# A two-layer graph network in one launch: order of first loads, place of the third dense product, chunks begun in hop 1, last chunks of hop 2 by halves

## The chip, the core and the metric

The kernel runs on one core of a Trainium2 chip. A core has five engines, each with an instruction queue of its own: TensorE (PE; its weight loads are listed as PEld), VectorE (DVE), ScalarE (ACT), GpSimd (POOL) and SyncE (SP), which here only issues DMAs. Sixteen DMA engines move data between HBM and the core's memories; SP, ACT and POOL issue to them. The metric is the device time of one launch in microseconds (us). The kernel before took 850.22 us, the median of three runs (850.05 to 854.02).

## The reference

x is [8, 2048, 128], adj is a 2048 x 2048 matrix R with about 0.4% of its entries nonzero (random pairs in both directions and the diagonal), all in fp32. Layer 0 computes, cut to what matters:

```
res = si[:, :, None] + sj[:, None, :] + R[None] * w_r + g_b     # si = x @ w_i, sj = x @ w_j
x   = layernorm(x + einsum('bij,bjd->bid', res, x) @ weight + bias)
```

Layer 1 is a Chebyshev step with the same matrix given twice:

```
x1 = einsum('bnf,nw->bwf', x, R);  x2 = 2 * einsum('bnf,nw->bwf', x1, R) - x      # for A1 and for A2, both R
x  = layernorm(x + relu(concat([x, x1, x2, x1, x2]) @ Theta1 + bias))
```

## The kernel before

**Tiling.** The 2048 nodes are 16 chunks of 128, numbered 0 to 15. A chunk of x or of a result is a tile of 128 nodes by 8 x 128 columns (batches by features), 512 KB; a product into it takes two PSUM banks of 512 columns, a half of the batches each. Of the eight PSUM banks, 0 to 3 hold two pairs of sums that are taken in turn (`acc_pair`, line 321), 4 and 5 serve the third dense product (`acc2`) and other things, 6 and 7 take transposes in turn.

**Dense and listed rows.** Layer 0 is computed as R times Y, Y = x @ weight, plus terms of rank nine (`rank9`). For chunks 0 to 3 this product is dense: `full_rows` (lines 311 to 318) multiplies the transposed block rows of R, kept in `at4`, with Y, two matmuls of 512 columns per block, in the order `LAST` (line 308: 0 to 3, 8 to 15, 4 to 7). For the other twelve chunks R is sparse enough to work with lists: DVE finds for each chunk which groups of columns hold a nonzero, ranks them, and writes indices `idx`. A chunk then needs its own diagonal block ("own"), four gathers by rows of 32 ("T") and three of 64 and 128 ("H"). A gather is an indirect DMA that POOL issues, of 128 rows of 4 KB of Y (or later u, y), and the rows of R that belong to it are gathered too, from `rr_d`, into a staging buffer `st` of four slots (`get_job`, line 543); DVE masks them and copies them to `rct` and `rc` (`keep_job`, line 554). `next_job` (line 662) is a keep followed by a get, so a POOL gather into a slot waits for DVE to have kept what was there.

**First stage (lines 327 to 345).** R is read in 16 block rows of 1 MB through a ring of three slots in the order `R_ORDER`. For each, DVE reduces it to a mask (`mask_rows`), PE transposes its 16 blocks in groups of four, and ACT copies each group out of PSUM, scaled by w_r (`wr`). With every second block row a chunk of x is transposed (`x_t`), multiplied with weight and the two columns of g_w, all in the tile `wx` (`y_of`), and the dense products of chunks 0 and 1 advance by one block. The loads are issued by SP, in the order of the list `todo` (lines 196 to 202), by `pump` (line 216) as far as their slots are free. ACT issues the small constants at the top (`load_constants`, lines 115 to 124): ten DMAs for `wx` (two), `wr`, the scalar `gb`, the bias row `b0row` (four times), `b1bc`, and `th` with the five blocks of Theta1.

**Lists (lines 686 to 701 and 776 to 822).** The remaining eight chunks of x go through the same steps, with the list work between them; then the ranking of the second set of lists runs on DVE in eight rounds (`rounds2`), while PE does column sums and the rank-nine terms. `lists_end(1)` (line 796) turns the second lists into indices with small transposes on PE. After it DVE adds residuals to the sums of chunks 0 and 1 (`z_add`) and normalises them; the third dense product, in three pieces of 5, 6 and 5 blocks, follows; between the pieces DVE and POOL do `next_job`s, and `make_u` (line 647) transposes a normalised chunk and multiplies it with the combined Theta block for the inner hop, storing it to `u_d` by a DMA of ACT's. The fourth dense product follows in the same way, and hop 0 (lines 839 to 862), the listed rows of layer 0, chunk by chunk.

**The buffers of gathered rows.** After layer 0's dense products Y is no longer needed, and twelve of its chunks, `Y[:, LAST[:12]]` (line 709), become the slots of gathered rows, taken in turn. The first T gathers of hop 0 overwrite Y of chunks 0 to 3, so they wait until the fourth dense product has read those.

**Hops of layer 1 (lines 865 to 940).** With the two equal matrices, the two hops are y = x Th1 + R^T u (hop 1, from `u_d`, results stored to `y_d`) and out = layernorm(x + relu(x Th2 + R^T y + bias)) (hop 2). For a chunk, `begin` does the products with Theta (eight matmuls), the own block and the T rows; `listed(.., "H")` the H rows; `end` copies the sums out (hop 1), or, in hop 2, adds the transposed x, applies the relu and the layer norm on DVE and ACT, and stores by a DMA of ACT's, 512 KB. POOL issues gathers in the order: T of two chunks, then per chunk the H rows of this one and the T rows of the next. In hop 1 the H rows of the first chunk need all of u, with the last chunk's `make_u` (`between`).

**Order of the instructions.** Every instruction goes through a wrapper, `Tied` (line 72), that keeps the program's order on each engine, so all of them carry line 72 in the profile and are told apart by their tiles.

**Semaphores of the DMAs.** In the built program the DMAs that SP and ACT issue take eight completion semaphores in turn, and those that POOL issues take eight others. A DMA waits, on the queue that issues it, until the one eight before it has completed.

Of the kernel before, what the change touches and what calls it, by code (L numbers as in the profile page):

```python
# [18 lines left out]
def kernel(  # L19
# [22 lines left out]
    P = 128  # L42
# [71 lines left out]

    def load_constants():
        with nc.allow_non_contiguous_dma(reason="two columns of 128 numbers"):
            act.dma_start(out=wx[:, D:D + 2], in_=g_w[0:2 * D].rearrange("(t p) -> p t", p=P))
        act.dma_start(out=wx[:, 0:D], in_=weight)
        act.dma_start(out=wr, in_=g_w[2 * D:2 * D + 1][None, :].to_broadcast([P, 1]))
        act.dma_start(out=gb, in_=g_b[None, :].to_broadcast([P, 1]))  # L120
        for i in range(4):
            act.dma_start(out=b0row[:, i, :], in_=bias0[None, :])
        act.dma_start(out=b1bc[:, 0, :], in_=bias1[None, :].to_broadcast([P, D]))
        act.dma_start(out=th, in_=theta.rearrange("(m p) f -> p m f", p=P))

    ctx.enter_context(nc.allow_non_contiguous_dma(reason="512-byte rows of a block of 128 columns"))
    load_constants()
    epst = const.tile([P, 1], F32)
# [68 lines left out]
    for k in range(NC):  # L197
        todo.append(("a", k))
        if x_at(k) is not None:
            todo.append(("x", x_at(k)))  # L200
    todo += [("x", 8), ("s", 12), ("x", 9), ("s", 13), ("x", 10), ("x", 11), ("s", 14), ("x", 12)]
    todo += [("s", 15), ("x", 13), ("x", 14), ("x", 15)] + [("c", c) for c in T_ORDER]
# [13 lines left out]
    def pump():  # L216
        while todo:
            what, n = todo[0]
            if what == "a" and n < done["a"] + 3:
                sp.dma_start(out=am[n % 3], in_=adj[R_ORDER[n] * P:(R_ORDER[n] + 1) * P, :])  # L220
            elif what == "x" and n < done["x"] + 6:
                c = X_ORDER[n]
                xin[c] = load_x(c, ring[:, X_SLOT[n % 6]])
                if c < ND:
                    zs[c] = xin[c]
            elif what == "s" and done["a"] == NC:
                store_rt(n)
            elif what == "c" and done["a"] == NC:
                copies([n])
            else:  # L230
                return
            todo.pop(0)
# [92 lines left out]

    acc0, acc1 = acc_pair(), acc_pair()
    pump()
    for k, n in enumerate(R_ORDER):
        m = x_at(k)
# [464 lines left out]
    next_job()  # L794
    rounds2([7])
    lists_end(1)
    z_add(acc0, zs[0])
# [3 lines left out]

    acc2 = bank[4:6]
    full_rows(2, acc2, LAST[:5])
    next_job()
    next_job()
    make_u(0, zs[0], x1t[0], u_of[0], 0)
    layernorm(zs[1], "0_1")
    full_rows(2, acc2, LAST[5:11])
    next_job()
    make_u(1, zs[1], x1t[1], u_of[1], 0)  # L810
    next_job()
    full_rows(2, acc2, LAST[11:])
    si_t(2)
    rank9(2, acc2)
    z_add(acc2, zs[2])
    overflow()
    next_job()
    layernorm(zs[2], "0_2")
# [46 lines left out]
    def hop(i, src, order, there, between):  # L865
        def theta_rows(c):
            accs = acc_pair()
            for h in range(2):
# [7 lines left out]
        def end(c, accs):  # L876
# [13 lines left out]
            else:  # L890
# [3 lines left out]
                )  # L894

        def fetch(k):
            if k < NC:
                load_own(i, src, order[k], homes[order[k]], order[k] in there)

        def begin(k):  # L900
            accs.append(theta_rows(order[k]))
            own_rows(i, order[k], accs[k], False)
            listed(i, order[k], accs[k], "T")
# [9 lines left out]
        rows(1, "T")  # L913
        begin(0)
        between()
        begin(1)
        for k, c in enumerate(order):
            rows(k, "H")
            if k > 1:
                begin(k)  # L920
            fetch(k + 2)
            if k > 0:
                rows(k + 1, "T")
# [111 lines left out]
```

## Time and profile before

| what | value |
|---|---|
| timed runs, median (three) | 850.22 us (850.05 to 854.02) |
| the profiled execution's own time | 818.08 us |
| its span (first to last instruction) | 816.3 us |
| mean granted TensorE clock | 0.971 |
| busy: PE, PEld, DVE, ACT, POOL | 90%, 45%, 48%, 24%, 55% of the span |
| DMA: bytes, mean rate | 253.90 MB, 311 GB/s |

How to read it: times are microseconds from the start of the span, means of one instruction are nanoseconds. The profile shows one execution, and the timed runs are other executions, 32 us longer in the median. "Busy" is the share of the span in which an engine executed something; issuing a DMA doesn't count. The chain of work that ended last is followed back from the last instruction, at each step to what released it. In a group or a line of the timeline, the bracket holds the idle time before it and what ended that. A timeline line gives start, length, engine, operation, output and inputs. A DMA's share is a mean over the sixteen engines.

The stages of this execution, from the timeline:

| stage | from | to |
|---|---|---|
| first loads; PE waits for the first x | 0 | 16.48 |
| R in 16 block rows, 12.41 us for two of them with one x | 16.48 | 109.5 |
| last x chunks, lists | 109.5 | 206 |
| third dense product ends | | 232.7 |
| fourth dense product ends | | 262 |
| hop 0 | 275 | 425 |
| hop 1 | 425 | 614 |
| hop 2, with the last store landed at 814.25 | 614 | 816.3 |

### The profile page before, as it was taken

Reading aid. Unit: us, or ns where it says so; the run is one execution under the profiler, and the core shown is the slowest. Engines: PE = TensorE matmul, PEld = TensorE weight load, DVE = VectorE, ACT = ScalarE, POOL = GpSimd, SP = SyncE. Lnnn points to the kernel's source line nnn. Section 1 sums busy time; section 2 is a strip of 40 time slices with the busy share of each in tenths; the row PEclk is TensorE's granted clock in tenths of the full one; section 3 lists DMA queues with packets and bytes.
Section 4 is the critical chain, followed back from the end, with each engine's and each line's share of the span. In section 5 each row is a group of like instructions: output and inputs, shape, how many; then the busy total and the mean of one; then the engine's idle time right before and its main releaser. Section 6 shows DMA issues by size and latency. Waiting matters only on the chain.

```text
span 816.3 us, 10067 instructions
## 1 busy us (share of the span) xinstructions
PE 732.8 (90%) x3554; PEld 364.9 (45%) x3554; DVE 394.7 (48%) x591; ACT 192.7 (24%) x439; POOL 445.2 (55%) x432
## 2 busy tenths in 40 slices
PE   4999999997999998988798888898899999999992
PEld 4666566642644343434345243333344454444441
DVE  4664876578341655555533000000100377777775
ACT  3757554321200332313222000000000011111101
POOL 1000000477747876776344677776774777776740
PEclk9999999997999999999899899999999999999997
DMA  8999999999326799999969799899999799999982
GB/s 264 296 314 316 352 292 295 314 398 347 119 89 223 244 346 368 341 344 367 356 224 344 246 364 360 314 365 346 339 372 357 252 343 357 370 385 389 363 299 68
DMA packets 165299, 253.90 MB, mean 311 GB/s; under 512 B 17255, under 2 KB 118020, under 8 KB 163192
## 3 DMA queue, kind: packets, MB, share of 16 engines
q0 software_dynamic: 49280, 146.52, 49.7%
q1 hardware_dynamic: 93200, 81.01, 31.1%
q10 hardware_dynamic: 22760, 25.63, 8.9%
q8 instruction: 30, 0.49, 0.2%
q14 instruction: 29, 0.24, 0.1%
HBM read 234.82 MB, written 58.72 MB: 360 GB/s over the span
## 4 chain that ended last, share of the span: by engine, by line
PE 52%; DMA 29%; issue 6%; ACT 6%; DVE 3%; POOL 2%; ACTq 0%; POOLq 0%; SPq 0%; DVEq 0%
PE bank L72 52%; DMA Y<-u_d,idx 12%; DMA Y<-y_d,idx 8%; DMA st<-rr_d,idx 2%; DMA rd<-rr_d 2%; ACT Y L72 2%; DMA ring<-in_x_dram 2%; POOL Y L72 1%; ACT rct L72 1%; ACT trp L72 1%; DMA trp<-in_adj_dram,idr 1%; DVE s L72 1%; DVE ring L72 1%; ACT at L72 1%; DVE st L72 1%
## 5 line engine op out<-in xcount | busy, mean ns | idle before, releaser
L72 POOL DMA_INDIRECT Y<-y_d,idx x196 | 212.0, 1081 | 93.2 <-PE bank L72 38.0
L72 PE MATMUL bank<-Y,rc 128*32 128x512 f32 (+2 forms) x896 | 219.7, 618 | 21.3 <-DMA Y<-u_d,idx 19.1
L72 POOL DMA_INDIRECT st<-rr_d,idx x84 | 90.3, 1075 | 183.5 <-DVE rown L72 148.3
L72 POOL DMA_INDIRECT Y<-u_d,idx x112 | 111.8, 999 | 53.9 <-issue 29.9
L72 PEld LDWEIGHTS bank<-Y,rc 128*32 128x32 f32 (+2 forms) x896 | 58.6, 130 | 179.3 <-issue 99.5
L72 PE MATMUL bank<-Y,at 128*128 128x512 f32 x256 | 115.2, 601 | 0.0
L72 PE MATMUL bank<-Y,rct 128*32 128x512 f32 (+2 forms) x336 | 77.3, 625 | 8.5 <-DMA Y<-y_d,idx 8.5
L72 DVE TENSOR_REDUCE s<-sq 128x4 f32<-128x512 f32 x64 | 43.9, 686 | 58.0 <-ACT sq L72 58.0
L72 PEld LDWEIGHTS bank<-Y,at 128*128 128x128 f32 x256 | 47.8, 193 | 53.6 <-issue 53.4
L72 DVE COPY ring<-bank 128x512 f32<-128x512 f32 x10 | 6.9, 692 | 110.1 <-PE bank L72 110.1
L72 ACT ACTIVATE sq<-ring 128x512 f32<-128x512 f32 x44 | 27.7, 630 | 129.5 <-DVE ring L72 109.7
L72 PE MATMUL bank<-ring,rd 128*128 128x512 f32 x108 | 51.5, 599 | 5.7 <-DMA rd<-rr_d 4.1
L72 PE MATMUL bank<-ident,rc 128*128 128x128 f32 (+2 forms) x302 | 45.0, 297 | 12.6 <-DMA rc<-in_adj_dram 6.6
L72 PE MATMUL bank<-th,at 128*128 128x128 f32 x384 | 49.2, 283 | 1.9 <-ACT at L72 1.9
L72 PEld LDWEIGHTS bank<-th,at 128*128 128x128 f32 x384 | 46.8, 197 | 6.7 <-ACT at L72 3.8
L72 DVE TENSOR_TENSOR ring<-bank,ring 128x512 f32<-128x512 f32 x26 | 17.3, 688 | 66.0 <-PE bank L72 60.8
L72 DVE TENSOR_REDUCE st<-rc 128x64 f32<-128x2048 f32 x16 | 36.5, 2283 | 25.7 <-DMA rc<-in_adj_dram 25.7
L72 ACT COPY ring<-bank 128x512 f32<-128x512 f32 x34 | 19.9, 586 | 122.5 <-PE bank L72 112.9
L72 PEld LDWEIGHTS bank<-Y,rct 128*32 128x32 f32 (+2 forms) x336 | 20.8, 130 | 57.3 <-issue 32.4
L72 PEld LDWEIGHTS bank<-ident,rc 128*128 128x128 f32 (+2 forms) x302 | 33.8, 150 | 25.5 <-issue 9.1
L72 PE MATMUL bank<-wx,trp 128*128 128x130 f32 x256 | 36.9, 288 | 4.3 <-ACT trp L72 2.2
L72 PE MATMUL bank<-ident,ring 128*128 128x128 f32 x232 | 32.5, 282 | 6.4 <-DMA ring<-in_x_dram 2.8
(142 smaller groups left out, 789.1 us busy)
## 6 DMA issues: line engine op xcount, KB each, us to landing
rc<-in_adj_dram SPq DMA_DIRECT2D x16, 1024.0 KB, 10.9
ring<-in_x_dram SPq DMA_DIRECT2D x25, 512.0 KB, 8.5
rr_d<-in_adj_dram SPq DMA_DIRECT2D x12, 1024.0 KB, 10.8
rr_d<-Y SPq DMA_DIRECT2D x8, 1024.0 KB, 9.0
y_d<-Y SPq DMA_DIRECT2D x16, 512.0 KB, 10.6
u_d<-ring ACTq DMA_DIRECT2D x12, 512.0 KB, 7.0
ring<-y_d SPq DMA_DIRECT2D x11, 512.0 KB, 23.2
ring<-u_d SPq DMA_DIRECT2D x10, 512.0 KB, 3.9
```

The source lines that it names most:

```text
L72: return lambda *a, **k: tc.keep_in_program_order(f(*a, **k))
```

## The change

Four edits, none of which changes what is computed.

- **First loads.** The constants are issued after the first `pump`, so SP's first loads of R and x come first in the program. ACT issues four of them, `wr` first. The other six (four times `b0row`, `b1bc`, `th`) go to SP, in the `todo` list between the last R and the ninth x.
- **Third product.** Two of its 16 blocks are placed ahead of `lists_end(1)`; the pieces after it are 7, 5 and 2 blocks instead of 5, 6 and 5. The `next_job` after the product moves ahead of `z_add(acc2)`.
- **Hop 1.** The T gathers of the third chunk are issued before `between` (the last `make_u`), and the third chunk is begun in banks 4 and 5, after the second; so at the first chunk's H rows three chunks are begun instead of two. The gathers and fetches that follow are renumbered so that the order is the old one from there on.
- **Hop 2.** For the last two chunks, `begin`, `listed` and `end` are replaced by `by_halves`: for each half of the batches the transposes, Theta products, own, T and H rows, then DVE's steps of this half (`begun_half`) and the normalisation and store of the half before (`ended_half`); a store is 256 KB.

```diff
@@ -113,18 +113,19 @@
     th = const.tile([P, 5, D], F32)
 
     def load_constants():
+        act.dma_start(out=wr, in_=g_w[2 * D:2 * D + 1][None, :].to_broadcast([P, 1]))
         with nc.allow_non_contiguous_dma(reason="two columns of 128 numbers"):
             act.dma_start(out=wx[:, D:D + 2], in_=g_w[0:2 * D].rearrange("(t p) -> p t", p=P))
         act.dma_start(out=wx[:, 0:D], in_=weight)
-        act.dma_start(out=wr, in_=g_w[2 * D:2 * D + 1][None, :].to_broadcast([P, 1]))
         act.dma_start(out=gb, in_=g_b[None, :].to_broadcast([P, 1]))
+
+    def load_later_constants():
         for i in range(4):
-            act.dma_start(out=b0row[:, i, :], in_=bias0[None, :])
-        act.dma_start(out=b1bc[:, 0, :], in_=bias1[None, :].to_broadcast([P, D]))
-        act.dma_start(out=th, in_=theta.rearrange("(m p) f -> p m f", p=P))
+            sp.dma_start(out=b0row[:, i, :], in_=bias0[None, :])
+        sp.dma_start(out=b1bc[:, 0, :], in_=bias1[None, :].to_broadcast([P, D]))
+        sp.dma_start(out=th, in_=theta.rearrange("(m p) f -> p m f", p=P))
 
     ctx.enter_context(nc.allow_non_contiguous_dma(reason="512-byte rows of a block of 128 columns"))
-    load_constants()
     epst = const.tile([P, 1], F32)
     dve.memset(epst, EPS)
     ones = const.tile([P, P], F32)
@@ -198,7 +199,7 @@
         todo.append(("a", k))
         if x_at(k) is not None:
             todo.append(("x", x_at(k)))
-    todo += [("x", 8), ("s", 12), ("x", 9), ("s", 13), ("x", 10), ("x", 11), ("s", 14), ("x", 12)]
+    todo += [("k", 0), ("x", 8), ("s", 12), ("x", 9), ("s", 13), ("x", 10), ("x", 11), ("s", 14), ("x", 12)]
     todo += [("s", 15), ("x", 13), ("x", 14), ("x", 15)] + [("c", c) for c in T_ORDER]
     done = {"a": 0, "x": 0}
 
@@ -223,6 +224,8 @@
                 xin[c] = load_x(c, ring[:, X_SLOT[n % 6]])
                 if c < ND:
                     zs[c] = xin[c]
+            elif what == "k":
+                load_later_constants()
             elif what == "s" and done["a"] == NC:
                 store_rt(n)
             elif what == "c" and done["a"] == NC:
@@ -325,6 +328,7 @@
 
     acc0, acc1 = acc_pair(), acc_pair()
     pump()
+    load_constants()
     for k, n in enumerate(R_ORDER):
         m = x_at(k)
         mask_rows(k)
@@ -793,28 +797,29 @@
     rounds2([5, 6])
     next_job()
     rounds2([7])
+    acc2 = bank[4:6]
+    full_rows(2, acc2, LAST[:2])
     lists_end(1)
     z_add(acc0, zs[0])
     z_add(acc1, zs[1])
     next_job()
     layernorm(zs[0], "0_0")
 
-    acc2 = bank[4:6]
-    full_rows(2, acc2, LAST[:5])
+    full_rows(2, acc2, LAST[2:9])
     next_job()
     next_job()
     make_u(0, zs[0], x1t[0], u_of[0], 0)
     layernorm(zs[1], "0_1")
-    full_rows(2, acc2, LAST[5:11])
+    full_rows(2, acc2, LAST[9:14])
     next_job()
     make_u(1, zs[1], x1t[1], u_of[1], 0)
     next_job()
-    full_rows(2, acc2, LAST[11:])
+    full_rows(2, acc2, LAST[14:])
     si_t(2)
     rank9(2, acc2)
+    next_job()
     z_add(acc2, zs[2])
     overflow()
-    next_job()
     layernorm(zs[2], "0_2")
 
     acc3 = bank[2:4]
@@ -863,8 +868,8 @@
 
 
     def hop(i, src, order, there, between):
-        def theta_rows(c):
-            accs = acc_pair()
+        def theta_rows(c, at=None):
+            accs = at or acc_pair()
             for h in range(2):
                 for b in range(HB):
                     pe.matmul(
@@ -893,12 +898,76 @@
                     out=out[:, c * P:(c + 1) * P, :].rearrange("b p f -> p b f"), in_=z
                 )
 
+        def begun_half(z, acc, b, h, s):
+            hs_ = slice(h * HB, (h + 1) * HB)
+            zh = z[:, hs_, :]
+            dve.tensor_add(zh, by4(acc), b1bc.to_broadcast([P, HB, D]))
+            dve.scalar_tensor_tensor(zh, zh, 0.0, b, op0=ALU.max, op1=ALU.add)
+            dve.tensor_reduce(s[:, 0, hs_], zh, AX.X, ALU.add)
+            dve.tensor_scalar(s[:, 1, hs_], s[:, 0, hs_], 1.0 / D, None, op0=ALU.mult)
+            dve.tensor_sub(zh, zh, s[:, 1, hs_][:, :, None].to_broadcast([P, HB, D]))
+            sq = small.tile([P, HB, D], F32, name=f"sqh{h}", tag="sq", bufs=1)
+            act.activation(sq, zh, AF.Square)
+            return zh, sq
+
+        def ended_half(c, zh, sq, h, s):
+            hs_ = slice(h * HB, (h + 1) * HB)
+            dve.tensor_reduce(s[:, 2, hs_], sq, AX.X, ALU.add)
+            act.activation(s[:, 3, hs_], s[:, 2, hs_], AF.Sqrt, bias=epst, scale=1.0 / D)
+            dve.reciprocal(s[:, 0, hs_], s[:, 3, hs_])
+            dve.tensor_mul(zh, zh, s[:, 0, hs_][:, :, None].to_broadcast([P, HB, D]))
+            act.dma_start(
+                out=out[hs_, c * P:(c + 1) * P, :].rearrange("b p f -> p b f"), in_=zh
+            )
+
+        halves = []
+
+        def by_halves(k):
+
+
+            c = order[k]
+            t, r = own.pop((i, c))
+            rcc = rc[:, c * W:(c + 1) * W]
+            accs = acc_pair()
+            s = small.tile([P, 4, B], F32, name=f"s_h{c}", tag="s")
+            for h in range(2):
+                lo, hi = h * 512, (h + 1) * 512
+                hs_ = slice(h * HB, (h + 1) * HB)
+                b = transposes([x1t[c][:, h * HB + n, :] for n in range(HB)])
+                for n in range(HB):
+                    pe.matmul(
+                        accs[h][:, n * P:(n + 1) * P], x1t[c][:, h * HB + n, :], th[:, i, :],
+                        start=(n == 0), stop=False, skip_group_check=True,
+                    )
+                pe.matmul(
+                    accs[h], r, t[:, hs_, :].rearrange("p b f -> p (b f)"), start=False, stop=False,
+                    skip_group_check=True,
+                )
+                for what, n, w in (("T", QT, TW), ("H", 2, 64)):
+                    for m in range(n):
+                        at = P * (what == "H") + w * m
+                        pe.matmul(
+                            accs[h][w * m:w * m + w], rcc[:, at:at + w],
+                            rows_of[i, c, what, m][:, lo:hi], start=False, stop=False,
+                            skip_group_check=True, tile_position=(0, w * m),
+                        )
+                pe.matmul(
+                    accs[h], rcc[:, 2 * P:3 * P], rows_of[i, c, "H", 2][:, lo:hi], start=False,
+                    stop=True, skip_group_check=True,
+                )
+                zh, sq = begun_half(homes[c], accs[h], b, h, s)
+                if halves:
+                    ended_half(*halves.pop())
+                halves.append((c, zh, sq, h, s))
+            if k == NC - 1:
+                ended_half(*halves.pop())
+
         def fetch(k):
             if k < NC:
                 load_own(i, src, order[k], homes[order[k]], order[k] in there)
 
-        def begin(k):
-            accs.append(theta_rows(order[k]))
+        def begin(k, at=None):
+            accs.append(theta_rows(order[k], at))
             own_rows(i, order[k], accs[k], False)
             listed(i, order[k], accs[k], "T")
 
@@ -912,14 +981,26 @@
         rows(0, "T")
         rows(1, "T")
         begin(0)
+        if i == 1:
+            fetch(2)
+            rows(2, "T")
         between()
         begin(1)
+        if i == 1:
+            begin(2, bank[4:6])
+        begun = len(accs)
         for k, c in enumerate(order):
+            if i == 2 and k >= NC - 2:
+                rows(k, "H")
+                rows(k + 1 if k + 1 < NC else NC, "T")
+                by_halves(k)
+                continue
             rows(k, "H")
-            if k > 1:
+            if k >= begun:
                 begin(k)
-            fetch(k + 2)
-            if k > 0:
+            if k + 2 >= begun:
+                fetch(k + 2)
+            if k + 1 >= begun:
                 rows(k + 1, "T")
             if i == 1 and (k % 2 and k < 12 or k == 12):
                 keep_job()
```

## The prediction

> **What bounds the kernel now.** I read the page first (busy shares, slices, the chain of work that ended last), then the waits of SP's queue, the chain in order of time, and the engines' timelines around the four places that the diff touches.
>
> ```profile
> PE 732.8 (90%) x3554; PEld 364.9 (45%) x3554; DVE 394.7 (48%) x591; ACT 192.7 (24%) x439; POOL 445.2 (55%) x432
> PE 52%; DMA 29%; issue 6%; ACT 6%; DVE 3%; POOL 2%; ACTq 0%; POOLq 0%; SPq 0%; DVEq 0%
> ```
>
> No engine bounds the whole. TensorE carries half of the chain, transfers 29%, and they take turns by stage. Busy time by stretch (us; then busy time and instructions of PE, PEld, DVE, ACT and POOL; clock, DMA share, GB/s):
>
> ```profile
> 0.00:20.00 20.00, 9.36 (x40) 7.89 (x41) 9.67 (x29) 7.07 (x10) 2.82 (x12) 1.00 0.81 263
> 20.00:110.00 90.00, 82.36 (x470) 55.83 (x470) 59.58 (x33) 57.02 (x136) 0.00 (x0) 1.00 1.02 315
> 190.00:233.00 43.00, 39.11 (x124) 20.59 (x125) 18.06 (x39) 9.15 (x16) 28.33 (x26) 0.90 0.54 176
> 640.00:752.00 112.00, 111.98 (x580) 54.40 (x576) 85.93 (x118) 16.52 (x32) 86.25 (x77) 1.00 1.00 360
> ```
>
> In the first 20 us PE works less than half the time. From 20 on PE and the DMA engines are both full. At 190 to 233 the DMA engines are half idle and the clock is 0.90. In the middle of hop 2 (last line) DMA is full.
>
> The start: SP's wait, then the chain's first pieces (start, length, what):
>
> ```profile
> SPq L72 <- DMA wx<-in_L_gnn_g_w_dram: 4.9, 1, 4.9
> ...
> 2.24 4.28 DMA gb<-in_L_gnn_g_b_dram
> 6.54 9.81 DMA ring<-in_x_dram
> 16.48 5.10 PE bank L72 x24
> ```
>
> SP's second load of R waits 4.9 us for a constant of ACT's queue, and the first x waits for gb. These are not data waits: the built program lets the DMAs of SP and ACT take eight completion semaphores in turn, and one waits until the transfer eight before it has landed. PE gets x at 16.48.
>
> The lists, from the timelines of PE and POOL (start, length, operation; idle before it and releaser):
>
> ```profile
> 191.20 0.46 PE L72 MATMUL bank<-ident,lists 96*64 96x48 f32 x4 [3.46 <-DVE lists L72]
> 191.58 10.61 PE L72 MATMUL bank<-Y,at 128*128 128x512 f32 x20
> 204.06 1.09 PE L72 MATMUL bank<-ident,ring 128*128 128x128 f32 x8 [1.87 <-DVE ring L72]
> ...
> 222.36 8.75 PE L72 MATMUL bank<-Y,at 128*128 128x512 f32 x20
> ...
> 234.74 1.00 POOL L72 DMA_INDIRECT st<-rr_d,idx  x1 [8.79 <-DVE rc L72]
> ```
>
> PE stands 3.46 and 1.87 us, and the same 20 records take 10.61 us after the first pause but 8.75 later. POOL stands 8.79 us for a keep that DVE has queued behind z_add of the third product.
>
> The start of hop 1, POOL and PE:
>
> ```profile
> 447.43 0.99 POOL L72 DMA_INDIRECT Y<-u_d,idx  x1 [6.85 <-DMA u_d<-st]
> 460.76 1.00 POOL L72 DMA_INDIRECT trp<-in_adj_dram,idr  x1 [3.29 <-DVE rc L72]
> 451.66 11.68 PE L72 MATMUL bank<-Y,rc 128*64 128x512 f32 x24 [4.58 <-DMA Y<-u_d,idx]
> ```
>
> The end, PEld, DVE and ACT's queue:
>
> ```profile
> 788.43 0.30 PEld L72 LDWEIGHTS bank<-Y,rc 128*128 128x128 f32 x2 [0.81 <-DMA Y<-y_d,idx]
> 789.59 0.69 DVE L72 TENSOR_TENSOR st<-bank,b1bc 128x512 f32<-128x512 f32 x1 [0.30 <-PE bank L72]
> 809.62 1.23 DVE L72 TENSOR_TENSOR st<-st,rs 128x1024 f32<-128x1024 f32 x1
> 810.87 0.38 ACTq L72 DMA_DIRECT2D out_dram<-st  x1
> ```
>
> The last chunk but one waits for its H rows until 788.43; DVE needs about 10.7 us a chunk, PE 10 to 11.6.
>
> **What the skill says.** The Trainium skill, "DMA: Bandwidth & Descriptors", "Queues, rings and completion order": on each DMA engine descriptors are consumed in ring order, so R0, R1, x, R2 on SP's queue should land in that order. The same page, "Anatomy of one DMA": DMA engines do not wait on semaphores; the wait is on the issuing sequencer. The 4.9 us on SPq agrees. "TensorE: Matmul & The Clock Gate", Part 1: after an idle window of about 3.4 us the array runs at half clock, and needs a busy window to recover. The trace agrees: records of 512 columns last 1061 ns at 192.6 and 592 at 196.
>
> **The start.** SP now issues R0, R1, x and R2 with no wait, 0.4 us each, by 2.5. R0 landed at 5.84 before and will again. At 360 GB/s (the full stretch above) R1, 1.05 MB, takes 2.9 us and x, 0.52 MB, 1.5: x is there at 10.2; I add 1 for the constants that share the engines and x's 512-byte rows: 11.2. ACT: four issues instead of eleven, which ended at 7.04; then wr must land (issue 0.75 plus the 4.6 that it took) and the table load, 1.28: first copy at 6.6, before 8.37. Six copies of R at the later pace of 0.72 end at 11. So PE takes x at about 11.2 instead of 16.48: 5.2 us. From 20 to 110 PE pays a steady 12.41 us per pair of R, so the lead lasts if the loads keep up. They began the full stretch at about 27 us and all start earlier with PE; but a late R has only half a microsecond to spare (the reduction of the fourteenth R starts at 86.95, PE is ready for it at about 87.5), and 0.4 MB of constants come back later: I take 4.7, between 2 and 6.
>
> The six moved constants stand on SP ahead of the ninth x. By the built program each waits for a transfer eight before it, and that x for the last R, which landed at 96.72 (its reduction's start). In ring order the other waits have ended by then. Shifted, x is issued at about 91.5 and lands 8.5 us later (median of its row), at 100; PE wants it at 109.51, shifted 104.3. Hidden, with 4 us of cover. th is wanted at 147.78, the bias rows at 181, far later.
>
> **The third product.** Four matmuls (two blocks, two halves) move into the gap at 187.7 to 191.2. Eight records take 3.5 us at full clock, up to 6.9 at half, and part of that place is half clock (the records before it took 1056 ns). So lists_end comes 0 to 2 us later, with DVE's chain. Then 14 matmuls at 0.87 last 12.2 us: PE reaches z of chunk 0 (before 204.06) just when it is ready. Gained: 3.46 and 1.87 idle; 1.9 of half clock in the block of 191.58; 1.6 in the Theta product at 205.39 (3.5 us against 1.9 later). Lost: about 2.3 for half clock where the block now stands. Sum 6.5, between 4 and 8. The product ends at about 226 in the old time instead of 232.7. POOL: the keep moves ahead of z_add, so the 8.79 us go. T rows of chunk 4 overwrite Y[0] to Y[3], free 1.7 to 7 us after the fourth product starts, so POOL follows PE's lead, not its own: 6.5. POOL's order is otherwise the same up to hop 1.
>
> **Hop 1.** The place where H rows of chunk 0 start, 447.43, is set by the store of u of chunk 15 and doesn't move relative to hop 0. Before it POOL had issued two of the four T rows of the third chunk; now all four: 2 x 1.30 us. PE has 5.6 us of the third chunk (1.95 + 1.88 + 1.92) to do in its gap of 4.58, which ends the half clock that follows, so chunk 0 ends about 2 us sooner and with it the keep for which POOL stood 3.29. In all POOL reaches T rows of the fourth chunk 4 us sooner, between 1 and 5.5: its 1.30 us per gather set the pace of this stage. From there the order is the old one.
>
> **The end.** The work of PE and the bytes are the same. A half needs its H rows 3.7 us into the chunk instead of 5.5. They come at 788.43 at the latest, so the first half of chunk 14 ends at about 789 and PE is 3.5 us late, since nothing covers the wait. DVE was free only at 789.2, and per half needs 5.0 us (0.79 + 0.72 + 0.72 + 0.21 + 0.61, then 1.05 + 0.24 + 0.61 and a little). Four halves of PE at 5.0 from 789 end at 804.3; DVE then needs 3.05 + 1.96 + 2: its last product ends at 811.3, before 810.85. The last store is half as long, about 0.8 us. Gain 0.3, between -3 and 2.5. The Square of one half and the sums of the half before share one buffer; the program puts no wait there.
>
> **Sum.** 4.7 + 6.5 + 4.0 + 0.3 = 15.5 us. Own time of the profiled execution: 818.08 with a span of 816.3; the span falls to about 801. The median of the timed runs is 32 us above the profiled one; I carry the difference over unchanged: 850.2 - 15.5 = 834.7.
>
> **Rivals.** (1) The DMA engines are the bound: share 1.02 from 20 to 110, full in hop 0 and hop 2. Then only filled idle counts: 2 at the start, 3 of the third product, 2 in hop 1: 843. For it: R's small slack. Against: PE's steady beat, and idle DMA engines (0.54) at 190 to 233, which let a lead pass. (2) The lead of the start and of POOL is eaten by the first wait that doesn't move: 849, no difference. Against it: I find no such wait; each stage begins with data of the one before. (3) Slower: the moved constants. If their six waits on SP do not overlap but come one after the other at 8 to 10 us, the ninth x lands near 150, PE stands 45 us, and the kernel takes 880. It decides from about 20 us beyond the cover. Against it: ring order.
>
> **Chances.** My forecast with its own range of 829 to 840: 0.62; better still, 0.05; rival 1, with milder losses, 840 to 846: 0.19; no difference: 0.09; slower: 0.05. What a measurement can tell from no change is 0.5%, 4.3 us: faster 0.86, same 0.09, slower 0.05. Range 828 to 847.
>
> **What would show it.** First x transposes at about 11 and the beat of 12.41 after it; no idle of more than 1 us at the lists; no 8.79 on POOL; PE busy from 440 to 453; the final store issued 14 to 16 us sooner. Wrong if PE waits for R between 20 and 110, if the ninth x is waited for, or if PE's waits for H rows in the last two chunks pass 5 us.

## The result

The changed kernel takes 861.56 us (median of 22 runs, 853.94 to 872.12) where the kernel before takes 852.83 (22 runs, 849.01 to 870.88): a ratio of 1.0078, 95% interval 1.0051 to 1.0105. That is 6.7 us slower. The ratio leaves out the runs that lie more than 1.5% above the fastest of their kernel, so it is smaller than that of the two medians, which are 8.7 us apart. I had forecast 834.7 with a range of 828 to 847, so the forecast was wrong in size and in sign.

One thing has to be said before any number below can be read. The kernel before took 848.60, 852.83 and 855.27 us in three sets of runs and 810.24, 810.93 and 811.25 in three others, and the sets don't overlap (844.31 and more against 818.92 and less). The profile that the prediction was worked out on, 818.08 us, is of the second kind, while the 850.22 beside it are of the first. Ratios below compare kernels within one set. I call the two kinds late and prompt sets, for a reason that the traces show.

The page of the changed kernel, in a late set (its own time 853.94, span 852.2, clock 0.948), engine shares and the chain:

```profile
PE 745.6 (87%) x3554; PEld 369.9 (43%) x3554; DVE 395.0 (46%) x601; ACT 193.6 (23%) x441; POOL 440.0 (52%) x432
PE 67%; issue 11%; DMA 9%; ACT 6%; DVE 2%; POOL 2%; another core or an unknown queue 1%; POOLq 0%; ACTq 0%; DVEq 0%
```

The DMA share of the chain has gone from 29% to 9%; "issue" and an unknown queue, work that the profile can't name, have 12% instead of 6%. The stretches that the prediction showed of before (columns as there):

```profile
0.00:20.00 20.00, 11.28 (x68) 9.16 (x68) 13.11 (x30) 10.38 (x21) 2.82 (x12) 1.00 0.90 303
20.00:110.00 90.00, 82.38 (x466) 55.15 (x465) 60.59 (x36) 56.58 (x138) 0.00 (x0) 1.00 1.01 316
190.00:233.00 43.00, 37.84 (x130) 16.56 (x123) 28.42 (x54) 9.49 (x17) 24.43 (x24) 0.88 0.52 165
640.00:752.00 112.00, 105.60 (x542) 49.80 (x541) 60.73 (x84) 12.10 (x23) 77.10 (x71) 0.98 0.93 324
```

The first 20 us hold 68 PE instructions instead of 40, and from 20 to 110 PE is as busy as before. What was lost lies later. PE's timeline at the places where it stands longest:

```profile
13.48 1.23 PE L72 MATMUL bank<-ident,ring 128*128 128x128 f32 x8 [0.32 <-ACT at L72]
161.05 1.16 PE L72 MATMUL bank<-wx,trp 128*128 128x130 f32 x8 [3.19 <-issue]
166.54 1.23 PE L72 MATMUL bank<-wx,trp 128*128 128x130 f32 x4 [4.33 <-ACT sraw L72]
172.92 1.24 PE L72 MATMUL bank<-wx,trp 128*128 128x130 f32 x4 [5.15 <-issue]
249.06 2.08 PE L72 MATMUL bank<-ub,sit 5*128 5x512 f32 x4 [7.38 <-ACT sit L72]
```

The first x is transposed at 13.48 instead of 16.48, and at the ninth x the lead is 4.5 us (104.99 against 109.51). Between 157 and 176 us it is gone: 12.7 us of idle in three places, where the profile of before has none. At 249 PE waits 7.38 us for a small copy of ACT's. The first question is whether the change made these waits.

### The profile page after: what moved, and what is told of

The parts are those of the page before. It is cut to its first block, busy times and chain, and to the rows that moved or that the text cites. A ratio compares the mean times of both kernels' runs of the same rounds, so it can differ in the third digit from the quotient of the medians.

```text
span 852.2 us, 10089 instructions
## 1 busy us (share of the span) xinstructions
PE 745.6 (87%) x3554; PEld 369.9 (43%) x3554; DVE 395.0 (46%) x601; ACT 193.6 (23%) x441; POOL 440.0 (52%) x432
## 4 chain that ended last, share of the span: by engine, by line
PE 67%; issue 11%; DMA 9%; ACT 6%; DVE 2%; POOL 2%; another core or an unknown queue 1%; POOLq 0%; ACTq 0%; DVEq 0%
PE bank L72 67%; DMA Y<-y_d,idx 5%; DMA Y<-u_d,idx 2%; ACT Y L72 2%; POOL Y L72 2%; ACT trp L72 1%; ACT rct L72 1%; ACT at L72 1%; DMA y_d<-st 1%; DVE st L72 1%; DMA wr<-in_L_gnn_g_w_dram 1%; DVE ring L72 1%; DVE s_h L72 0%; ACT L72 0%
## 5 line engine op out<-in xcount | busy, mean ns | idle before, releaser
L72 PE MATMUL bank<-Y,rc 128*32 128x512 f32 (+2 forms) x896 | 228.5, 624 | 24.6 <-issue 14.1
L72 POOL DMA_INDIRECT st<-rr_d,idx x84 | 86.3, 1027 | 190.4 <-DVE rown L72 143.7
L72 PE MATMUL bank<-Y,at 128*128 128x512 f32 x256 | 117.7, 612 | 0.0
L72 DVE TENSOR_REDUCE s<-sq 128x4 f32<-128x512 f32 x60 | 41.2, 686 | 82.8 <-ACT sq L72 48.0
L72 PE MATMUL bank<-Y,rct 128*32 128x512 f32 (+2 forms) x336 | 70.4, 624 | 0.0
L72 PE MATMUL bank<-ring,rd 128*128 128x512 f32 x108 | 54.1, 621 | 2.1 <-issue 2.0
L72 PEld LDWEIGHTS bank<-wx,trp 128*128 128x128 f32 x256 | 31.9, 194 | 22.0 <-ACT sraw L72 9.4
L72 PEld LDWEIGHTS bank<-Y,rct 128*32 128x32 f32 (+2 forms) x336 | 19.3, 130 | 43.3 <-issue 38.7
```

The costliest lines, as they stand in the source:

```text
L72: return lambda *a, **k: tc.keep_in_program_order(f(*a, **k))
```

## Experiments

**Is the first profile of before a usual one?** The kernel before, unchanged, was profiled again.

> The kernel before, unchanged, for a second profile. Theory A: its first profiled execution, 818.08 us beside a median of 850, was not a usual one, and the 32 us are waits that it lacks and that the changed kernel's trace has; then this profile has a span near 845 to 855, PE idle of 15 to 35 us between 110 and 290 us on waits for ACT or DVE, and an acc3 end near 275 instead of 260. Theory B: the change makes these waits; then this profile repeats the first one, 816 to 822 us, with PE idle of at most 4 us at any one place. The ratio to itself is 1.000 within its interval in both.

Ratio to itself 0.9996 (0.9961 to 1.0030); profiled span 859.6. PE, then ACT:

```profile
170.87 2.10 PE L72 MATMUL bank<-wx,trp 128*128 128x130 f32 x8 [8.43 <-issue]
181.25 2.10 PE L72 MATMUL bank<-wx,trp 128*128 128x130 f32 x8 [8.28 <-ACT sraw L72]
251.70 1.13 PE L72 MATMUL bank<-ub,sit 5*128 5x512 f32 x4 [0.35 <-ACT sit L72]
...
244.44 0.59 ACT L72 COPY ring<-bank 128x512 f32<-128x512 f32 x1 [3.00 <-remote]
247.98 0.59 ACT L72 COPY ring<-bank 128x512 f32<-128x512 f32 x1 [2.96 <-remote]
```

Theory A holds: the waits at the last x chunks (8.43 and 8.28 us here) belong to no edit. The span is 43.3 us longer than in the first profile, and PE is busy for 5.6 us of that (738.4 instead of 732.8) and idle for 37.7, so it is waiting that has grown, and a lower clock has little to do with it.

Since the program is the same as in the first profile, each of 792 waits of PE, ACT and DVE, for one another or for work of their own, can be laid beside its counterpart there. 40 of them end 0.8 to 13.6 us after the instruction that released them there, where they ended 0.04 to 0.1 us after it in the first profile. 39 of the 40 wait for PE (30 on ACT, 9 on DVE), of 253 waits for PE in all. At 38 of these 39 the trace has an update of PE's semaphore within 0.1 us of the wait's end, so it is PE that they waited for and not something else that came late. In the traces of the first loads alone and of hop 1 alone, below, 33 and 42 waits for PE are late in the same way. The two copies above are of this kind: PE's products end at 241.70 and 242.65. The Trainium skill, "Perfetto Trace Analysis", section "Per-instruction lifecycle: what the profiler-reported window actually captures", says that for TensorE the reported end is an estimate, and that the semaphore is pushed after PSUM has acknowledged the writes, outside the window shown. The traces agree: what is late lies between the shown end and the release. They can't tell a late end, a late write and a late semaphore apart, and I say late release for all three. In the trace of a prompt set (the one with halves alone) one such wait is left in the part of the program that is the same.

**One edit at a time, in a late set.** Each kernel is the kernel before with one of the four edits of the diff above.

> The first edit alone: constants after the first loads, six of them on SP's queue. Theory A (the usual execution has delays that belong to no edit, and the edit keeps its own gain): the ninth x is used 4.5 us sooner, 850 falls to 845 to 848, ratio 0.994 to 0.998. Theory B (the moved loads of constants cause the delays on ACT and DVE between 110 and 290 us): ratio 1.005 to 1.015.

> The second edit alone: third dense product around the lists, with the next keep ahead of its sum. By my prediction it gains 4 to 8 us: ratio 0.990 to 0.995. If the lists are delayed in the usual execution anyway, PE's idle place is longer than what the edit fills and the gain is the four matmuls alone, 2 us or less: 0.997 to 1.000. If the edit is what costs (lists_end starts later, with DVE's chain behind it): 1.005 to 1.010.

> The third edit alone: three chunks of hop 1 begun at once. By my prediction it gains 1 to 5.5 us: ratio 0.993 to 0.999. Rival: the T gathers of the third chunk stand on POOL ahead of the H gathers that end the first chunk, and the overlap is lost later: 1.000 to 1.008.

First loads 0.9956 (0.9919 to 0.9992), third product with its keep 1.0083 (1.0047 to 1.0118), hop 1 1.0056 (1.0024 to 1.0088). The first gains 3.8 us, the second loses 7.1, the third 4.8. Where the second loses (ACT, then PE):

```profile
248.33 0.59 ACT L72 COPY ring<-bank 128x512 f32<-128x512 f32 x1 [4.37 <-remote]
252.61 0.59 ACT L72 COPY ring<-bank 128x512 f32<-128x512 f32 x1 [3.69 <-remote]
254.79 0.26 ACT L72 COPY sit<-bank 37x128 f32<-37x128 f32 x1 [1.60 <-remote]
...
255.11 2.08 PE L72 MATMUL bank<-ub,sit 5*128 5x512 f32 x4 [6.38 <-ACT sit L72]
257.23 30.47 PE L72 MATMUL bank<-Y,at 128*128 128x512 f32 x64
```

Late copies of u stand in both kernels; in this one the second copy starts 7.43 us after PE's product, before 5.33. Before, five blocks of the third product (8.75 us) lie between make_u of chunk 1 and the transposed si of chunk 2, and PE waits 0.35 us. With the edit two blocks are left (3.60 us), PE comes early and stands 6.38 us behind ACT, and then runs at half clock (the granted clock is 0.5 from 252.5 to 262.8): the rank-nine product takes 2.08 us instead of 1.13, the fourth product 30.47 instead of 27.73. Together 9.7 us, all of the distance from the third product's end to the fourth's (39.1 us against 29.4).

**The second edit in its two halves, and the fourth alone.** This set turned out prompt. `third_blocks` leaves the keep behind the sum, `third_keep` moves the keep alone:

```diff
     rank9(2, acc2)
+    next_job()
     z_add(acc2, zs[2])
     overflow()
-    next_job()
```

`no_first_gathers`, in `get_job`, skips the gathers of four jobs, so rows of four chunks are missing from its result:

```diff
         for n, i in enumerate(columns(c, what)):
+            if got[0] <= 4:
+                continue
```

> The second edit without its moved keep: two blocks ahead of the lists, then pieces of 7, 5 and 2, but the keep and its gathers stay behind the sum of the third product. Theory C (cover): only two blocks are left between make_u of chunk 1 and the transposes of si, so PE catches up with ACT's late copies of u; the loss is in the pieces, and this kernel shows it in full: PE idle of 4 to 8 us before the rank-nine product, ratio 1.006 to 1.010. Theory D (gathers): the earlier keep lets POOL issue 20 gathers in one train instead of 15, and the late semaphores come with the train; then this kernel has no such idle and the ratio is 0.995 to 1.000.

> The moved keep alone: next_job ahead of the sum of the third product, its pieces as before (5, 6, 5). Theory C: five blocks cover ACT, no idle before the rank-nine product, and POOL's stall of 8.9 us is gone: 0.997 to 1.001. Theory D: the train of gathers is longer, PE idles there 3 us or more: 1.004 to 1.010.

> The fourth edit alone: last two chunks of hop 2 by halves. My prediction: gain 0.3 us, between -3 and 2.5, ratio 0.997 to 1.003. By the sum of what was measured (whole 1.0078; first, second and third edit alone 0.9956, 1.0083, 1.0056, which add up to 1.0095) it gains about 1.5 us: 0.998. Rival: in the usual execution the halves wait longer for their rows and it loses 3 to 5 us: 1.004 to 1.006; the second hop of the changed kernel, first T product to last product, is 3 us longer than in the kernel before (194.2 to 191.1).

> The kernel before, with the first four jobs' T gathers from rr_d (16 gathers of POOL at 150 to 175 us) left out, so the T rows of four listed chunks are not R's. It asks what goes with PE's late semaphores at 155 to 185 us, where the second profile has PE idle for 8.4 and 8.3 us. If they go with POOL's gathers, the two idles fall under 2 us and the time by 10 to 18 us: 0.979 to 0.988. If they go with SP's large copies or with the place alone, the idles stay and the ratio is 0.995 to 1.000.

Blocks alone 0.9919 (0.9891 to 0.9947), keep alone 0.9977 (0.9955 to 1.0000), halves 1.0033 (1.0009 to 1.0057), without the first gathers 1.0008 (0.9988 to 1.0027). The last one came to nothing: in a prompt set there are no late releases at its place to take away. Theories C and D could not be told apart here either, for the same reason: both forecasts for the blocks alone were made for a late set, and 0.9919 lies in neither. But the gain of the second edit is plain where releases are prompt.

The halves lose 2.7 us, a part of it by a wait that I had not priced. POOL in the kernel with halves alone, then PE in the third of the four halves:

```profile
776.02 1.51 POOL L72 DMA_INDIRECT Y<-y_d,idx  x1 [0.30 <-PE bank L72]
784.60 0.99 POOL L72 DMA_INDIRECT Y<-y_d,idx  x1 [7.07 <-PE bank L72]
785.89 0.99 POOL L72 DMA_INDIRECT Y<-y_d,idx  x1 [0.30 <-issue]
...
788.53 2.96 PE L72 MATMUL bank<-Y,rc 128*32 128x512 f32 x12
791.89 1.13 PE L72 MATMUL bank<-Y,rc 128*128 128x512 f32 x2 [0.40 <-DMA Y<-y_d,idx]
```

And in the kernel with the keep alone, whose end is that of the kernel before:

```profile
775.43 0.98 POOL L72 DMA_INDIRECT Y<-y_d,idx  x1 [0.35 <-PE bank L72]
776.81 0.98 POOL L72 DMA_INDIRECT Y<-y_d,idx  x1 [0.39 <-issue]
```

A slot of gathered rows is free when its last reader is done. By halves, the T rows of the last chunk but one are read until its second half, so the last two gathers of the kernel wait 7.07 us for slots. PE waits in turn for the rows that they bring: the third half takes 6.60 us where the second, which waits for nothing, takes 5.25. That is 1.35 of the 2.7 us (an estimate from this one trace). The first half takes 8.39 us, since its own H rows come late, but this wait was in the prediction, with 3.5 us.

**The whole change and its parts where releases are prompt.** `third_cover` is the second edit with pieces of 2, 5, 4 and 5 blocks.

> The changed kernel again. In the last runs the kernel before took 811 us and no wait for TensorE's semaphores was late; in the first ones and in the result it took 851 to 855 and they were 1 to 13 us late at 40 places. Theory E: the change's worth depends on that. Where the kernel before takes 811, the parts give 0.995 (first loads, 4.5 us), 0.990 (third product and keep, 8 us), 0.996 (hop 1, 3 us) and 1.003 (halves, measured): 0.982 to 0.988, 797 to 801 us. Where it takes 850: 1.008 again. Theory F: the change costs in both, 1.005 to 1.011.

> The second edit alone again (1.0083 where the kernel before took 855). Theory E: 0.988 to 0.992 where it takes 811 (blocks alone gave 0.9919, the keep alone 0.9977), 1.008 where it takes 850.

> The third edit alone again (1.0056 where the kernel before took 855). Theory E: 0.994 to 0.998 where it takes 811, as predicted from the first profile; 1.005 where it takes 850. Rival: a gain that is lost again in the same hop, 0.999 to 1.002 in both.

> The second edit with its pieces cut so that five blocks, not two, stay behind make_u of chunk 1 (2 ahead of the lists, then 5, 4, 5). Theory C: where semaphores are late this covers ACT's copies, and the loss of 0.8% turns into 0.994 to 1.000; where they are not late it is like the second edit alone within 0.3%, 0.988 to 0.993. If the pieces don't matter, it repeats only_third_2 in both.

Theory E holds for the whole change and for the second edit, but not for hop 1, which was to gain here and fits, in this set, its rival: a gain that is lost again in the same hop. The whole change: 799.06 us against 810.24, ratio 0.9876 (0.9831 to 0.9922), 10.0 us faster. The second edit alone 0.9886 (0.9848 to 0.9925), hop 1 1.0017 (0.9994 to 1.0040), `third_cover` 0.9971 (0.9955 to 0.9988). PE with the second edit alone, and then with `third_cover`:

```profile
193.57 12.28 PE L72 MATMUL bank<-Y,at 128*128 128x512 f32 x28
206.10 1.09 PE L72 MATMUL bank<-ident,ring 128*128 128x128 f32 x8 [0.25 <-DVE ring L72]
...
225.13 1.13 PE L72 MATMUL bank<-ub,sit 5*128 5x512 f32 x4 [0.35 <-ACT sit L72]
226.30 27.73 PE L72 MATMUL bank<-Y,at 128*128 128x512 f32 x64
```

```profile
191.64 8.85 PE L72 MATMUL bank<-Y,at 128*128 128x512 f32 x20
204.16 1.97 PE L72 MATMUL bank<-ident,ring 128*128 128x128 f32 x8 [3.67 <-DVE ring L72]
```

Seven blocks after the lists last until z of chunk 0 is ready. Five leave a hole of 3.67 us, and `third_cover` falls short of its forecast of 0.988 to 0.993. The seven are needed at one end and the last five at the other, and the product has only sixteen.

Hop 1, POOL in the kernel with the third edit alone:

```profile
446.45 0.98 POOL L72 DMA_INDIRECT Y<-u_d,idx  x1 [8.80 <-DMA u_d<-st]
460.56 1.00 POOL L72 DMA_INDIRECT trp<-in_adj_dram,idr  x1 [4.07 <-DVE rc L72]
```

And PE there:

```profile
448.34 1.90 PE L72 MATMUL bank<-Y,rc 128*32 128x512 f32 x10 [0.66 <-DMA Y<-u_d,idx]
451.78 1.07 PE L72 MATMUL bank<-Y,rc 128*64 128x512 f32 x2 [1.53 <-DMA Y<-u_d,idx]
454.12 10.89 PE L72 MATMUL bank<-Y,rc 128*64 128x512 f32 x30 [1.27 <-DMA Y<-u_d,idx]
```

With the old hop 1 (the kernel with the keep alone), POOL and PE:

```profile
441.46 0.99 POOL L72 DMA_INDIRECT Y<-u_d,idx  x1 [8.26 <-DMA u_d<-st]
453.98 1.00 POOL L72 DMA_INDIRECT trp<-in_adj_dram,idr  x1 [2.48 <-DVE rc L72]
...
445.74 10.83 PE L72 MATMUL bank<-Y,rc 128*64 128x512 f32 x24 [5.61 <-DMA Y<-u_d,idx]
```

With the edit PE waits 3.5 us in three parts instead of 5.61 at once, but the H rows come later. There are two prompt traces with the edit (`only_hop1_2` and `after_2`) and eleven without. The last H product of chunk 0 begins 10.9 and 11.1 us after POOL's first H gather, and 8.2 to 10.1 without. So chunk 0 ends later, not sooner, and POOL's stop for the keep is 4.07 and 4.45 us, and 1.32 to 3.90 without. From the issue of the last u's store to the first H gather it takes 8.2 and 7.9 us, and 3.0 to 7.0 without. That two more gathers were on the DMA engines ahead of that store may be the reason; it isn't shown.

**Once more, and the version that may beat both.** `third_725` is the second edit with pieces of 2, 7, 2 and 5 blocks; `start_third` has the first two edits only.

> The first and the second edit without the third and the fourth, as the version that may beat both. Where the kernel before takes 811: minus 4.3 (first loads) and minus 9.2 (third product) is 0.983, 797, against 0.9876 for the whole change. Where it takes 850 to 855: minus 3.8 and plus 7.1 is 1.004 if the second edit still loses there.

> The second edit without its moved keep, again (0.9919 where the kernel before took 811). Where it takes 850 to 855, theory C (two blocks left behind make_u of chunk 1 no longer cover ACT's late copies) gives the whole loss, 1.006 to 1.010; theory D (the longer train of gathers) gives 0.992 to 1.000. Where it takes 811 it repeats 0.992.

> The moved keep alone, again (0.9977 where the kernel before took 811). Where it takes 850 to 855, theory C gives 0.997 to 1.001, theory D 1.004 to 1.010. Where it takes 811 it repeats 0.998.

> The second edit with pieces of 2, 7, 2 and 5 blocks: seven stay behind the lists, five behind make_u of chunk 1, and the thin place moves ahead of make_u of chunk 1. Where the kernel before takes 850 to 855, theory C gives no loss if z of chunk 1 is ready in time, 0.992 to 1.000; theory D repeats the loss of the second edit, 1.006 to 1.010. Where it takes 811 the seven blocks keep PE busy until z of chunk 0 is ready, and it is near the second edit alone, 0.988 to 0.991.

Again a prompt set. `start_third` 0.9844 (0.9815 to 0.9872), 797.40 us against 810.93; blocks alone 0.9913 (0.9881 to 0.9944), keep alone 0.9984 (0.9969 to 1.0000), `third_725` 0.9950 (0.9929 to 0.9971): there PE waits 2.23 us for z of chunk 1, and the forecast of 0.988 to 0.991 was missed. The interval of `start_third` overlaps that of the whole change, so it isn't shown to be the faster of the two.

**ACT made late by hand.** Since the kind of set can't be chosen, the late copies were made by doing each copy of u of chunk 1 six times:

```diff
-            act.copy(u[:, h * HB:(h + 1) * HB, :], b)
+            for _ in range(6 if c == 1 else 1):
+                act.copy(u[:, h * HB:(h + 1) * HB, :], b)
```

> ACT made late by hand at the disputed place: in make_u of chunk 1 each of the two copies of u is done six times instead of once, 5.9 us more on ACT, in the kernel before. Here ACT stands idle 8.1 us before it copies the transposed si of chunk 2, so theory C expects nothing lost: 0.999 to 1.002, PE idle before the rank-nine product of chunk 2 under 1 us. If late copies cost by another way (the bank, the store of u), 1.004 to 1.008. Where the kernel before takes 850 to 855 it loses 3 to 6 us, since the cover is used up already.

> The same late copies with the second edit. Here ACT stands idle only 3.0 us before that copy, so theory C expects PE to idle 3 to 4 us before the rank-nine product, and a part of the fourth product at half clock, together 3 to 6 us against the second edit alone (0.9886): 0.993 to 0.997. If the short last piece doesn't matter: 0.987 to 0.991.

This set was late. Ratios 1.0110 (1.0056 to 1.0165) and 1.0165 (1.0113 to 1.0217). PE at the disputed place, in the kernel before with the copies, and then with the second edit too:

```profile
250.60 1.13 PE L72 MATMUL bank<-ub,sit 5*128 5x512 f32 x4 [0.35 <-ACT sit L72]
```

```profile
257.25 2.08 PE L72 MATMUL bank<-ub,sit 5*128 5x512 f32 x4 [8.78 <-ACT sit L72]
259.37 29.38 PE L72 MATMUL bank<-Y,at 128*128 128x512 f32 x64
```

With five blocks behind it even 5.9 us more of ACT cost nothing at this place; with two blocks PE stands 8.78 us, where theory C had 3 to 4, though for a prompt set. Over all seven late traces the wait is 0.35 us in the four without the second edit, and 6.38, 7.38 and 8.78 in the three with it. But the pieces are not all that differs: the two copies come 0.9 to 5.7 us late in sum in the four traces and 7.4 to 10.5 in the three. What the pieces account for can be estimated. Three blocks are 8.75 - 3.60 = 5.15 us of cover, and the three waits are 6.0, 7.0 and 8.4 us longer than 0.35. So theory C has the larger part of each, and 0.9 to 3.3 us go with the later copies. Theory D may be behind that rest. In all seven traces the second copy begins 0.1 to 2.4 us after the end of a train of POOL's gathers, which is 15 long in the four and 18 in the three. It is no more than a coincidence in time: the prompt traces have these gathers too and no late copy, and blocks and keep apart were never run in a late set. The copies also cost `before_copies` 9 us by its ratio (5 to 14), where I had 3 to 6 from a cover used up; the cover was not used up, so this place doesn't explain the cost, and that stays open.

The parts side by side:

| edit | late set | prompt set |
|---|---|---|
| first loads | 0.9956 | - |
| third product | 1.0083 | 0.9886 |
| hop 1 | 1.0056 | 1.0017 |
| halves | - | 1.0033 |
| all four | 1.0078 | 0.9876 |
| first loads and third product | - | 0.9844 |

## Why the prediction was wrong

**The step that failed: "the median of the timed runs is 32 us above the profiled one; I carry the difference over unchanged".** Those 32 us were not an offset around the same execution. The timed executions have late releases that the profiled one doesn't have, and the edits act on them. Where they are absent, the sum made for that profile went the right way: 15.5 us forecast, 10.0 measured (6.3 to 13.7). Where they are present, two of its terms turn over: the third product, forecast to gain 6.5 us, loses 7.1, and hop 1, forecast to gain 4.0, loses 4.8; the first loads keep their gain (4.7 forecast, 3.8 measured), and the end was not measured there. In the third product it is ACT's spare time behind make_u of chunk 1 that the sum had put at nothing. ACT stands idle there for 8.11 us in the first profile and for 2.96 in the prompt trace of the changed kernel, and late copies use that up:

```profile
231.26 0.26 ACT L72 COPY sit<-bank 37x128 f32<-37x128 f32 x1 [8.11 <-PE bank L72]
```

```profile
218.80 0.26 ACT L72 COPY sit<-bank 37x128 f32<-37x128 f32 x1 [2.96 <-DMA u_d<-ring]
```

(The second line names the store of u; PE's transposes end 0.04 us before it, as in the first.) None of the rivals had this in it; the difference of 32 us between profile and runs was the sign, and I read past it.

**The start** (4.7, between 2 and 6): right in size, in part by luck. The lead is 4.5 us at the ninth x in the late trace and 4.3 in the prompt one, 3.8 by the ratio. But at the first x, where I had 5.2, it is 3.0 and 3.5. PE in the profile of before, and then in the prompt trace of the changed kernel:

```profile
5.96 1.94 PE L72 MATMUL bank<-ident,rc 128*128 128x128 f32 x8 [5.96 <-DMA rc<-in_adj_dram]
16.48 1.94 PE L72 MATMUL bank<-ident,ring 128*128 128x128 f32 x8 [2.79 <-DMA ring<-in_x_dram]
```

```profile
7.50 1.94 PE L72 MATMUL bank<-ident,rc 128*128 128x128 f32 x8 [7.50 <-DMA rc<-in_adj_dram]
12.98 1.40 PE L72 MATMUL bank<-ident,ring 128*128 128x128 f32 x8
```

The first R, of which I had said that it lands as before, came 1.5 us later with more loads under way. `wr` landed 6.8 us after its issue instead of 4.6, and ACT's first scaled copy began at 8.91 instead of 6.6. So x, whose last packet came at 11.5 against the 11.2 that I had, waited for PE until 13.0. The rest of the lead comes from something that I had left out: before, the products after the wait for x are slow (eight transposes in 1.94 us), and without that wait they are not (1.40), which makes the lead 4.9 us at the second x; 0.6 of it goes again before the ninth. The moved constants cost nothing: all six were issued between 87.4 and 90.4 in that trace, 0.25 to 0.49 us each, and the ninth x landed at 97.4, against the 100 that I had. I had argued this from ring order; the section of the skill that I named also says that a later DMA may finish its writes before an earlier one, so the order of landing was a guess, and it held here. The rival of 880 fell. (ACT issued ten DMAs before, not eleven.)

**The third product** (6.5, between 4 and 8): right in mechanism in a prompt set, where it gains more than the range allows. The blocks alone are worth 6.6 and 7.1 us, the keep 1.9 and 1.3 (both intervals reach to nothing), blocks and keep together 9.2. I had credited POOL's 8.79 us with nothing of its own. In a late set the step "Lost: about 2.3 for half clock where the block now stands" was short: it priced the two blocks at their new place, and not the place behind make_u of chunk 1, where three blocks fewer now covered ACT. Of the swing of 16 us between the sets, 9.7 are located there; a second wait, for the si of chunk 4, costs some 1.6 more; the rest is not located. One reading of the trace was also off: the half clock at 192.6 had begun at 184.9, after a wait of 1.20 us, so this place shows the recovery of which the skill speaks, but not its idle window of about 3.4 us. The waits of 6.38 and 7.38 us in the late traces show that: the granted clock falls to 0.5 within each.

**Hop 1** (4.0, between 1 and 5.5): wrong, no gain in a prompt set but 1.4 us lost (0.5 gained to 3.2 lost, so not clear of nothing). Two premises failed. The place where H rows of chunk 0 start "is set by the store of u of chunk 15 and doesn't move relative to hop 0": it does wait for the store of u, but that store took 8.2 and 7.9 us, longer than in any prompt trace without the edit. And "so chunk 0 ends about 2 us sooner": PE's gap was shortened, but the H rows came later, so the end of chunk 0, its keep and POOL's stop moved back. POOL reaches the T rows of the fourth chunk 19.3 and 19.7 us after the first H gather, against 19.2 to 21.8 in the eleven traces without: about 1 us in the mean, not 4. In a late set the edit lost 4.8 us. From the first H gather to the last gather of the hop its two late traces take 172.5 and 173.9 us, the five without it 175.7 to 178.2, so it isn't lost there; where it is, stays open. (PE's work on the third chunk, 1.95 + 1.88 + 1.92, is 5.75 us and not 5.6, which changes nothing.)

**The end** (0.3, between -3 and 2.5): right within its range, at its lower end: 2.7 us lost. The step "They come at 788.43 at the latest", of the H rows, took the gathers' issue as unmoved, and the 7.07 us that POOL waits for slots weren't in it; PE's later end by about 1.35 us comes from there. PE's cost per half was right: 5.25 us for a half that waits for nothing, against the 5.0 that I took.

## What to carry over

When timed runs lie 4% above the profile, as here, the profile may show another kind of execution than the one that is timed: profile again until they agree, before any sum is made. Work moved into a gap leaves a gap where it stood, and what it covered there has to be priced with the same care as what it fills. And when a buffer gets a later last reader, ask at once which queue waits for that buffer.

## What the hardware showed unexpectedly

Releases by PE come within 0.04 to 0.1 us of the shown end of a product in one kind of set, and 0.8 to 13.6 us after it at 39 of 253 waits for PE in the other. It holds for whole sets of runs of the same program, whatever the edit, and the sets with it are some 40 us of 810 longer for the kernel before. What brings it about was not found. It isn't the chip alone: the record numbers the chip of each set after the result, and chip 7 ran a prompt set and, later, a late one. The one kernel meant to test POOL's gathers as its cause fell into a prompt set.
